# Three weight tables selected on VectorE in attention slots, and GpSimd's rotary sums ordered behind a slot's first scores

## The chip, the cores and the metric

The kernel runs on one core of a Trainium2 chip. Time is device time in microseconds (us) of one execution; the kernel before took 619.77 us, the median of three runs (619.49 to 621.18). A profiled execution of the same kernel took 619.1 us. All engine times below are from that execution, counted from the start of its span.

## The reference

Two transformer layers on a sequence tensor of 2 x 512 x 256, all in float32. Every sublayer is `x = x + layernorm(f(layernorm(x)))`:

```python
# layer 0: causal attention, 16 heads of 128, rotary embedding on q and k
q, k = rope(x @ wq.T + bq), rope(x @ wk.T + bk)
attn = softmax(where(causal, -inf, q @ k.T / sqrt(128)))
h = (attn @ v) @ wo.T + bo + residual
# layer 0 feed-forward, 256 -> 2048 -> 256: weights in 4-bit codes with a scale for each 32
W = NVFP4_LUT[codes] * scales;  out = (gelu(x @ Wg.T) * (x @ Wu.T)) @ Wd.T
# layer 1: linear attention with running sums over the sequence
out = q * cumsum(k * v) / (q * cumsum(k) + 1e-9) @ W_out.T / 4
# layer 1 feed-forward, 256 -> 688 -> 256: each weight is one of 16 values
w = lut[idx];  out = (silu(x @ wg.T) * (x @ wu.T)) @ wd.T
```

The change concerns the last line: the three tables `wg`, `wu`, `wd`, each `lut[idx]` with 16 possible values, have to be built on the chip from their index arrays before the last feed-forward.

## The kernel before, in words

**Stages.** Both batches of 512 positions are normalised (`first_norms`), then attention runs as 32 *slots*, one for each batch and head (`slot`, slot i is head i mod 16 of batch i div 16). After slot 17 and after slot 33 the sums over heads are finished and normalised; then come the first feed-forward for four units of 256 positions (`ffn_hidden`, `ffn_out`), linear attention (`linear_attention`) and the last feed-forward (`silu_hidden`, `silu_out`). Slots 30 to 33 already carry parts of the first `ffn_hidden`.

**What a slot does.** On TensorE (PE), in this order: the scores of head i, the projections of q and k for head i + 2, the output projection of head i - 2, the product of turned probabilities and values for head i - 1 (`attended`), and values for later heads. On VectorE (DVE): four reductions with the mask (`scores`, which writes the row minima `mn` and copies the scores into `p`), then the rotary products of q (`ra`, `ry`), the reciprocal of the row sums, the rotary product `ry` of k, and the four transposes of `p` into `turned`. On ScalarE (ACT): four exponentials, then `ra` of k, then the scaling of `p` by the reciprocals (four `p<-p,rs`), then two small copies that prepare a later slot's PSUM, then `oT` and `v`. On GpSimd (POOL): the sums `qT`, `kT` of the head after this one, and `ra*cos` of k. From slot 5 on, q and k of a head are projected two slots ahead, and their sums are made one slot ahead; for heads below 5 all is nearer together, and slot 3 makes the projections of k for head 4 and of q and k for head 5.

**Queues.** SyncE (SP) issues every DMA, in program order, each waiting in that queue for its own inputs. In a slot these are weight loads (`load`), the halves of `ry` exchanged into `rr`, and four DMAs `pT<-turned`, which bring the turned probabilities into place and can't start before `attended` of the slot has finished reading `pT` (one buffer).

**Dequantisation.** Twelve jobs turn 4-bit codes into weights of the first feed-forward (`dequantised`): a load of the codes `pk` (256 KB) and of the scales `sc`; then three steps, put into `behind` and taken out one at a time by `catch_up`: ACT casts `pk` to bytes `p8`; DVE separates the bits; DVE multiplies by the scales. Before the change the loads are issued in the middle of an even slot (from slot 2), the cast comes at that slot's end, the bits early in the next slot behind the scores, and the product at its end.

**The tables.** `wg` is built by `look_up_in`: for each of two pieces of 752 columns and 16 values, DVE makes `(idx == i) * lut[i]` and POOL adds it to the table; one such term per slot and a few more late. `wu` and `wd` are built by `select_in`, on DVE alone: for each piece 19 steps, which are 4 bit masks, 8 pairs (one of two table words by the lowest bit) and 7 predicated copies. `wu` (5 pieces of 256 columns) starts at slot 17, `wd` (3 pieces of 512) behind attention. These steps are *fills*: the recording layer `Engine` keeps a rough model of when each engine is busy, and where the model sees DVE idle ahead of its next instruction, it puts fills in front of that instruction; `flush` writes all that are left.

The order of instructions on each engine is thus fixed when the program is recorded: by the order of the code, by `poll` and `catch_up`, and by the model for the fills. On the chip every engine takes its instructions in that order.

Of the kernel before, what the change touches and what calls it, by code (L numbers as in the profile page):

```python
# [10 lines left out]
F32 = mybir.dt.float32  # L11
I32 = mybir.dt.int32
# [5 lines left out]
ALU = mybir.AluOpType  # L18

P = 128  # L20
HALF = P // 2
B = 2
S = 512
D = 256
# [18 lines left out]
SWAPPED = (1, 2)  # L43
WARM = 9
FROM = 5
REST = INTER - (NO - 1) * P


# [53 lines left out]
class Engine:  # L102
# [32 lines left out]
    def fill(self, until):  # L135
        self.filling = True
        while self.fills:
            us, reads, write = self.fills[0]
            if self.busy + us > until or (reads is not None and self.times.written(reads) > self.busy):
                break  # L140
            self.fills.popleft()
            write()
        self.filling = False

    def flush(self):
# [47 lines left out]
def sandwich_kernel(  # L193
# [58 lines left out]
    def begin(chain, delay=0.0):  # L252
        chains.append([now[0] + delay, chain])
# [13 lines left out]
    def catch_up():  # L267
        if behind:
            behind.popleft()()
# [171 lines left out]
        yield 0.0 if (u, stage) == (2, 1) else until(to)  # L441


    terms = deque()

    def look_up_in(scratch, pieces):


        n = [to.shape[-1] for _, to in pieces]
        ix = [scratch[:, 3 + j % 2, : n[j]].bitcast(I32) for j in range(len(pieces))]  # L450

        def fetch(j):
            if j < len(pieces):
                sync.dma_start(out=ix[j], in_=pieces[j][0])

        fetch(0)

        def term(j, i):
            if i == 2:
                fetch(j + 1)  # L460
            to = pieces[j][1]
            e = to if i == 0 else scratch[:, i % 3, : n[j]]
            vector.tensor_scalar(
                e, ix[j], float(i), lut_sb[:, i : i + 1], ALU.is_equal, ALU.mult
            )
            if i:
                pool.tensor_add(to, to, e)

        terms.extend(lambda j=j, i=i: term(j, i) for j in range(len(pieces)) for i in range(16))

    def select_in(scratch, pieces):


# [50 lines left out]
        fetch(0)  # L524
        for j in range(len(pieces)):
            vector.fills.extend(piece(j))

    def look_up(n):
        for _ in range(min(n, len(terms))):
            terms.popleft()()  # L530


    wg_u, wu_u, wd_u = [], [], []
    xT1 = [None] * NUNIT
    with ExitStack() as at:
# [319 lines left out]
            jobs.append((down_p, down_s, u, "d", w))  # L855
            wd_u.append(w)

        scratch = fh.tile([P, 5, wg.shape[-1]], F32, tag="hT", name="scratch", bufs=1)
        look_up_in(scratch, [(gate_i[:, kc, :], wg[:, kc, :]) for kc in range(NK)])
        words = lut_sb.bitcast(I32).rearrange("p (i j) -> p i j", j=2)  # L860

        p_at = [0, 128, 384, 768]
# [13 lines left out]
        def projection(kind, i, tag="mm"):  # L876


            b, h = divmod(i, NH)
            gg, hh = divmod(i, HG)  # L880
            w = wts[kind, gg]
            bias = col(kind, h)
            a = qk.tile([P, S], F32, tag="ra", name="ra", bufs=4)
            r = qk.tile([P, S], F32, tag="rr", name="rr", bufs=3)
            to = qk.tile([P, S], F32, tag=f"T{kind}", name=f"{kind}T", bufs=3)
            lo, hi = slice(0, 64), slice(64, 128)

            if i >= FROM:
                ps = bank(tag)
                for kc in range(NK):  # L890
                    matmul(
                        ps,
                        w[:, hh, kc, :],
                        chunk(xT0[b], kc) if b else xT0[b][:, kc, :],
                        kc == 0,
                        kc == NK - 1,
                    )
                yield
                y = qk.tile([P, S], F32, tag="ry", name="ry")
                if kind == "q":  # L900
                    vector.scalar_tensor_tensor(a, ps, bias, cos_sb, ALU.add, ALU.mult)
                else:
                    scalar.activation(a, ps, AF.Identity, bias=bias)
                    pool.tensor_mul(a, a, cos_sb)
                vector.scalar_tensor_tensor(y, ps, bias, sin_sb, ALU.add, ALU.mult)
                for half, other in ((lo, hi), (hi, lo)):
                    sync.dma_start(out=r[half], in_=y[other])
                yield
                pool.tensor_add(to, a, r)
                (qT if kind == "q" else kT)[i] = to  # L910
                return


            for cs in [slice(0, TU), slice(TU, S)] if i == 0 else [slice(0, S)]:
                ps = bank(tag)
                first_half = i == 0 and cs.start == 0
                tiles = [slice(0, P), slice(P, TU)] if first_half and kind == "q" else [cs]
                for n, (ts, kc) in enumerate((ts, kc) for ts in tiles for kc in range(NK)):
                    matmul(
                        ps[:, ts],  # L920
                        w[:, hh, kc, :],
                        chunk(xT0[b], kc) if b else xT0[b][:, kc, ts],
                        kc == 0,
                        kc == NK - 1,
                    )
                    if first_half and (kind, n) in (("q", 1), ("k", 0)):
                        yield
                yield
                def by_scalar():
                    scalar.activation(a[:, cs], ps[:, cs], AF.Identity, bias=bias)  # L930
                    pool.tensor_mul(a[:, cs], a[:, cs], cos_sb[:, cs])


                if i and (kind == "k") == (i > 1):
                    by_scalar()
                elif not first_half:
                    vector.scalar_tensor_tensor(
                        a[:, cs], ps[:, cs], bias, cos_sb[:, cs], ALU.add, ALU.mult
                    )
                vector.scalar_tensor_tensor(  # L940
                    r[lo, cs], ps[hi, cs], bias[hi], sin_sb[hi, cs], ALU.add, ALU.mult
                )
                vector.scalar_tensor_tensor(
                    r[hi, cs], ps[lo, cs], bias[lo], sin_sb[lo, cs], ALU.add, ALU.mult
                )
                if first_half:
                    by_scalar()
            yield
            if (kind, i) == ("k", 1):
                inverted(0)  # L950
            (pool if i > 1 or kind == "q" else vector).tensor_add(to, a, r)
            (qT if kind == "q" else kT)[i] = to
# [223 lines left out]
        def slot(i):  # L1176
# [11 lines left out]
                load("k", (i + 3) // 2)  # L1188
            if i == 4:
                vector.tensor_tensor(differ, words[:, :, 0], words[:, :, 1], ALU.bitwise_xor)  # L1190
            if i == NH + 2:
                attention_sums(0)
                begin(after_attention(0))
            if i == NH + 1:

                flat = [
                    [t.rearrange("p k c -> p (k c)") for t in (up_i, wu)],
                    [t[0].rearrange("p k s -> p (k s)") for t in (xT0, xTv)],
                ]
                parts = [[t[:, at : at + TU] for at in range(0, t.shape[-1], TU)] for t in flat[1]]  # L1200
                select_in(
                    parts[0] + parts[1],
                    [tuple(t[:, at : at + TU] for t in flat[0]) for at in range(0, NK * FULL * P, TU)],
                )
            now_in, done = i < NS, not (jobs or behind)
            if now_in:
                ps_p[i] = (
                    pr.tile([P, 1280], F32, tag="p", name="p"),
# [28 lines left out]
                exps(i, 2)  # L1237
                exps(i, 0)
                exps(i, 1)
            catch_up()  # L1240
            if i < NS - 2:
                look_up(i > 0)
            else:
                assert not terms
            turning = []
            if FROM <= i + 1 < NS:
                for kind in "qk":
                    next(begun.pop((kind, i + 1)), None)
            for kind in "qk":
                if kind == "q" and i in (0, 2, 3):  # L1250
                    pass
# [11 lines left out]
                elif i <= NS:  # L1263
                    next(main)
                    next(main)
                if kind == "q" and jobs and i % 2 == 0 and i >= 2:
                    dequantised(*jobs.popleft())
                if kind == "q" and i and now_in:
                    inverted(i)
            for work in turning:  # L1270
# [38 lines left out]
            elif NS - 2 < i <= NS:  # L1309
                next(main)  # L1310
                next(main)
            poll()
            if i < NS - 2:
                look_up(done)
            catch_up()

        pair = projection("q", 0), projection("k", 0, "o")
        for rows, cs, base in (
# [27 lines left out]
        for i in range(NS + 2):  # L1346
            slot(i)
        attention_sums(1)
        begin(after_attention(1))


# [8 lines left out]
    wout_sb = lw.tile([P, NK, D], F32, name="wout_sb")  # L1360
    sync.dma_start(out=wout_sb, in_=wout)
    carry = {}
    scratch = lw.tile([P, 8, 2 * D], F32, name="scratch2")
    vector.flush()
    select_in(
        [scratch[:, j] for j in range(8)],
        [
            tuple(t[:, o : o + 2, :].rearrange("p o d -> p (o d)") for t in (down_i, wd))
            for o in range(0, NO, 2)
        ],  # L1370
    )

    def linear_attention(u):
        def flat(t):
# [306 lines left out]
```

## Time and profile before

| what | us |
|---|---|
| time, median of three runs | 619.77 |
| time of the profiled execution | 619.1 |
| its span | 617.3 |
| PE busy | 610.4 (99% of the span) |
| DVE busy | 441.0 (71%) |
| ACT busy | 306.5 (50%) |
| POOL busy | 279.3 (45%) |
| POOL adding terms to `wg` | 53.7 (30 of 1.79 each) |
| DVE making those terms | 19.3 (32 of 0.604 each) |

The span is what the profiler records; the execution's own time is 1.8 us more. A busy time counts the union of an engine's instructions; they overlap a little, so the step from one start to the next is shorter than the duration of one. In the tables of groups, each line names an engine, an operation, `out<-in` by tile names, the count and the mean of one. In a timeline each line is `start, duration, engine, line, operation, out<-in`, and in brackets the idle time ahead of it and what ended it.

### The profile page before, as it was taken

What the parts mean: (1) busy time and instruction counts of PE and PEld (TensorE: products, weight loads), DVE (VectorE), ACT (ScalarE), POOL (GpSimd) and SP (SyncE); (2) the same over time, 40 slices, a digit from 0 to 9 for tenths busy, and PEclk for the clock granted to TensorE, in tenths of its full rate; (3) what the DMA queues carried; (4) which work ended last, traced back from release to release, by engine and by line L of the source; (5) the groups of instructions that cost most, each with busy time, mean ns of one, the idle gap of its engine ahead of it and who ended that gap; (6) DMA issues with size and microseconds to landing.
All of it is one profiled execution on the core that took longest, in us unless ns stands there. A gap on an engine that the chain in (4) does not pass through costs nothing.

```text
span 617.3 us, 13497 instructions
## 1 busy us (share of the span) xinstructions
PE 610.4 (99%) x4968; PEld 455.4 (74%) x4968; DVE 441.0 (71%) x1115; ACT 306.5 (50%) x716; POOL 279.3 (45%) x346
## 2 busy tenths in 40 slices
PE   9999999999999999999999999999999999999996
PEld 6455565555555566666777999999999999996664
DVE  7987778667665887887866788778986751562963
ACT  5665776677565666666656562132324223325110
POOL 6354666537456275675667300350261350161531
PEclk9999999999999999999999999999999999999999
DMA  8476777787877888788775432211001000001010
GB/s 224 141 199 171 206 191 201 193 234 199 196 214 194 202 212 194 189 216 215 192 169 138 101 70 60 104 36 35 1 8 31 1 18 18 2 1 35 19 53 18
DMA packets 53104, 75.60 MB, mean 122 GB/s; under 512 B 6960, under 2 KB 34096, under 8 KB 53040
## 3 DMA queue, kind: packets, MB, share of 16 engines
q1 hardware_dynamic: 53040, 74.76, 47.5%
q8 instruction: 39, 0.64, 0.4%
q14 instruction: 25, 0.20, 0.1%
HBM read 28.59 MB, written 1.05 MB: 48 GB/s over the span
## 4 chain that ended last, share of the span: by engine, by line
PE 97%; DVE 2%; ACT 1%; DMA 0%; issue 0%; POOL 0%; DVEq 0%
PE ps_mm L284 39%; PE ps_o L284 22%; PE ps_s L284 21%; PE ps_t L284 14%; DVE rr L185 0%; ACT p L185 0%; DMA x<-in_x_turned 0%; DVE p L185 0%; DVE x L185 0%; POOL rstd L185 0%; DVE st L185 0%; DVE ra L185 0%; DVE centred L185 0%; ACT ra L185 0%; DVE wg L185 0%
## 5 line engine op out<-in xcount | busy, mean ns | idle before, releaser
L185 POOL TENSOR_TENSOR wg<-wg,scratch 128x752 f32<-128x752 f32 x30 | 53.7, 1791 | 105.8 <-DVE scratch L185 74.1
L284 PE MATMUL ps_mm<-xT,wg 128*64 128x256 f32 (+1 forms) x704 | 89.0, 379 | 0.0
L284 PE MATMUL ps_s<-xT,wu 128*64 128x256 f32 x672 | 85.0, 379 | 0.0
L185 ACT ACTIVATE p<-p,mn 128x512 f32<-128x512 f32 (+3 forms) x128 | 70.3, 550 | 26.9 <-DVE mn L185 26.9
L284 PE MATMUL ps_o<-wd,hT 128*64 128x256 f32 (+1 forms) x704 | 77.1, 375 | 0.0
L284 PE MATMUL ps_t<-pT,v 128*64 128x256 f32 (+3 forms) x512 | 75.5, 432 | 0.0
L284 PEld LDWEIGHTS ps_mm<-xT,wg 128*64 128x64 f32 (+1 forms) x704 | 71.2, 137 | 5.6 <-ACT si L185 0.4
L284 PEld LDWEIGHTS ps_o<-wd,hT 128*64 128x64 f32 x704 | 68.8, 137 | 6.3
L284 PEld LDWEIGHTS ps_s<-xT,wu 128*64 128x64 f32 x672 | 69.0, 137 | 4.5 <-DVE hT L185 0.3
L185 DVE CUSTOM_DVE_ANT_0 p<-ps_s,mask 128x512 f32<-128x512 f32 x64 | 31.3, 489 | 52.6 <-PE ps_s L284 49.3
L284 PEld LDWEIGHTS ps_t<-pT,v 128*64 128x64 f32 x512 | 45.9, 137 | 30.8 <-issue 22.4
L185 ACT ACTIVATE p<-p,rs 128x512 f32<-128x512 f32 (+3 forms) x128 | 61.1, 550 | 2.4 <-DVE rs L185 2.4
L284 PE MATMUL ps_o<-wo,oT 128*64 128x256 f32 x512 | 62.0, 379 | 0.0
L284 PEld LDWEIGHTS ps_o<-wo,oT 128*64 128x64 f32 x512 | 46.2, 137 | 21.1 <-issue 14.2
L284 PE MATMUL ps_mm<-xT,wk 128*64 128x512 f32 x248 | 59.4, 592 | 1.0 <-DVE rr L185 1.0
L284 PE MATMUL ps_mm<-xT,wq 128*64 128x512 f32 (+2 forms) x256 | 59.9, 577 | 0.1
L284 PE MATMUL ps_s<-kT,qT 128*64 128x64 f32 (+5 forms) x384 | 57.1, 424 | 0.0
L284 PE MATMUL ps_mm<-wv,xTv 128*64 128x256 f32 x464 | 55.9, 379 | 0.0
L185 DVE SCALAR_TENSOR_TENSOR ry<-ps_mm,cols_sb,sin_sb 128x512 f32<-128x512 f32 x54 | 40.3, 746 | 20.7 <-ACT ra L185 20.7
L185 DVE STREAM_TRANSPOSE turned<-p 128x512 f32<-128x512 f32 (+3 forms) x128 | 53.8, 476 | 0.3 <-ACT p L185 0.2
L185 POOL TENSOR_TENSOR ra<-ra,cos_sb 128x512 f32<-128x512 f32 (+1 forms) x33 | 46.0, 1395 | 16.5 <-ACT ra L185 16.5
L284 PEld LDWEIGHTS ps_s<-kT,qT 128*64 128x64 f32 x384 | 34.8, 137 | 23.7 <-issue 13.1
(162 smaller groups left out, 951.1 us busy)
## 6 DMA issues: line engine op xcount, KB each, us to landing
pT<-turned SPq DMA_DIRECT2D x128, 208.0 KB, 4.0
rr<-ry SPq DMA_DIRECT2D x108, 128.0 KB, 2.5
wo<-in_wo SPq DMA_DIRECT2D x17, 256.0 KB, 4.2
wv<-in_wv SPq DMA_DIRECT2D x16, 256.0 KB, 3.9
wq<-in_wq SPq DMA_DIRECT2D x15, 256.0 KB, 4.2
wk<-in_wk SPq DMA_DIRECT2D x15, 256.0 KB, 4.5
xT<-tr SPq DMA_DIRECT2D x48, 64.0 KB, 2.1
pk_g<-in_gate_p SPq DMA_DIRECT2D x4, 256.0 KB, 3.7
```

What stands on the lines that cost most here:

```text
L185: return write(*args, **more)
L284: nc.tensor.matmul(out[part], lhsT=lhsT[:, part], rhs=rhs, start=start, stop=stop, **more)
```

## The change

`look_up_in` and its terms on POOL are gone. All three tables go through `select_in`: `wg` and `wu` from slot 4 on in pieces of up to 512 columns (three for `wg`, three for `wu`), with a scratch tile of 8 x 512; `wd` from the end of slot 28 in six pieces of 256, with tiles of the first batch as scratch. Besides the places that the model sees as idle, fills are now forced at the end of each slot until the model's DVE is busy to 2.4 us beyond the model's time (`force`, `AHEAD`), and what is left is flushed at the end of slot 28 and behind attention. The loads of a dequantisation job and its steps move: loads at the end of an even slot, cast behind the next slot's exponentials (`if len(behind) == 3`), bits at the end of that slot, product at the end of the slot after. On POOL a small instruction that reads the first reduction's `mn` stands ahead of the two sums. `ra` has three buffers and not four.

```diff
+AHEAD = 2.4
...
+    def force(self, until):
+        self.filling = True
+        while self.fills and self.busy + self.fills[0][0] <= until:
+            self.fills.popleft()[2]()
+        self.filling = False
...
-    terms = deque()
-
-    def look_up_in(scratch, pieces):
...
-            vector.tensor_scalar(
-                e, ix[j], float(i), lut_sb[:, i : i + 1], ALU.is_equal, ALU.mult
-            )
-            if i:
-                pool.tensor_add(to, to, e)
...
-        scratch = fh.tile([P, 5, wg.shape[-1]], F32, tag="hT", name="scratch", bufs=1)
-        look_up_in(scratch, [(gate_i[:, kc, :], wg[:, kc, :]) for kc in range(NK)])
...
-            a = qk.tile([P, S], F32, tag="ra", name="ra", bufs=4)
+            a = qk.tile([P, S], F32, tag="ra", name="ra", bufs=3)
...
             if i == 4:
                 vector.tensor_tensor(differ, words[:, :, 0], words[:, :, 1], ALU.bitwise_xor)
+                scratch = fh.tile([P, 8, S], F32, tag="hT", name="scratch", bufs=1)
+                pieces = []
+                for codes, to in ((gate_i, wg), (up_i, wu)):
+                    codes, to = (t.rearrange("p k c -> p (k c)") for t in (codes, to))
+                    n = to.shape[-1]
+                    pieces += [tuple(t[:, at : min(at + S, n)] for t in (codes, to)) for at in range(0, n, S)]
+                select_in([scratch[:, j] for j in range(8)], pieces)
...
-            if i == NH + 1:
...
-                select_in(
-                    parts[0] + parts[1],
-                    [tuple(t[:, at : at + TU] for t in flat[0]) for at in range(0, NK * FULL * P, TU)],
-                )
...
-            catch_up()
-            if i < NS - 2:
-                look_up(i > 0)
-            else:
-                assert not terms
-            turning = []
+            if len(behind) == 3:
+                catch_up()
             if FROM <= i + 1 < NS:
+                after = small.tile([P, 1], F32, tag="after", name="after", bufs=1)
+                pool.tensor_scalar(after, ps_p[i][1][:, NT - 1 :], 1.0, None, ALU.mult)
                 for kind in "qk":
                     next(begun.pop((kind, i + 1)), None)
+            turning = []
...
-                if kind == "q" and jobs and i % 2 == 0 and i >= 2:
-                    dequantised(*jobs.popleft())
...
             poll()
+            catch_up()
+            if jobs and i % 2 == 0 and i >= 2:
+                assert not behind
+                dequantised(*jobs.popleft())
             if i < NS - 2:
-                look_up(done)
-            catch_up()
+                vector.force(now[0] + AHEAD)
+            if i == NS - 4:
+                vector.flush()
+                flat = [t[0].rearrange("p k s -> p (k s)") for t in (xT0, xTv)]
+                select_in(
+                    [t[:, at : at + TU] for t in flat for at in range(0, t.shape[-1], TU)],
+                    [(down_i[:, o, :], wd[:, o, :]) for o in range(NO)],
+                )
...
+        vector.flush()
         begin(after_attention(1))
...
-    scratch = lw.tile([P, 8, 2 * D], F32, name="scratch2")
-    vector.flush()
-    select_in(
-        [scratch[:, j] for j in range(8)],
...
-    )
```

More of the change, by code (lines that the diff above doesn't have):

```diff
@@ L441, in norms @@
         yield 0.0 if (u, stage) == (2, 1) else until(to)
-    terms = deque()
-    def look_up_in(scratch, pieces):
[L449 to L462, printed above, removed]
-            vector.tensor_scalar(
-                e, ix[j], float(i), lut_sb[:, i : i + 1], ALU.is_equal, ALU.mult
-            )
-            if i:
-                pool.tensor_add(to, to, e)
-        terms.extend(lambda j=j, i=i: term(j, i) for j in range(len(pieces)) for i in range(16))
     def select_in(scratch, pieces):
@@ L526, in select_in @@
             vector.fills.extend(piece(j))
-    def look_up(n):
-        for _ in range(min(n, len(terms))):
-            terms.popleft()()
     wg_u, wu_u, wd_u = [], [], []
@@ L1193, in slot @@
                 begin(after_attention(0))
-            if i == NH + 1:
[L1196 to L1200, printed above, removed]
-                select_in(
-                    parts[0] + parts[1],
-                    [tuple(t[:, at : at + TU] for t in flat[0]) for at in range(0, NK * FULL * P, TU)],
-                )
-            now_in, done = i < NS, not (jobs or behind)
+            now_in = i < NS
             if now_in:
@@ L1362, in sandwich_kernel @@
     carry = {}
-    scratch = lw.tile([P, 8, 2 * D], F32, name="scratch2")
-    vector.flush()
-    select_in(
-        [scratch[:, j] for j in range(8)],
[L1367 to L1370, printed above, removed]
-    )
     def linear_attention(u):
```

## The prediction

> **What bounds the kernel now.** I read the page's busy times and the chain that ended last, then what PE waited for, then timelines of slots 3, 9, 10 and 25 on each engine, because the chain alone doesn't say how much room other engines have.
>
> ```profile
> PE 610.4 (99%) x4968; PEld 455.4 (74%) x4968; DVE 441.0 (71%) x1115; ACT 306.5 (50%) x716; POOL 279.3 (45%) x346
> ...
> PE 97%; DVE 2%; ACT 1%; DMA 0%; issue 0%; POOL 0%; DVEq 0%
> ...
> PE ps_mm L284 <- DVE rr L185: 1.0, 1, 1.0
> PE ps_o L581 <- PEq L1669: 0.8, 1, 0.8
> PE ps_t L284 <- ACT wu L185: 0.3, 1, 0.3
> ```
>
> PE is the bound. The last three lines are all that it ever waited for: 2.1 us, of which 1.0 is in slot 3. Freeing DVE or POOL can return almost nothing; the question is whether the new order makes PE wait. From slot 5 a slot takes 10.98 us; I count time in a slot from its first scores on PE. Slot 3, the one with the wait, in lines of the timelines of SP, ACT, DVE and PE, and the load's own time to landing:
>
> ```profile
> 45.08 0.60 SPq L167 DMA_DIRECT2D wq<-in_wq  x1
> ...
> wq<-in_wq SPq DMA_DIRECT2D x1, 256.0 KB, 4.0
> ...
> 44.05 0.62 ACT L185 CAST p<-pk_g 128x512 uint8<-128x512 int32 x1
> ...
> 47.35 0.67 ACT L185 ACTIVATE ra<-ps_mm,cols_sb 128x512 f32<-128x512 f32 x1
> ...
> 48.12 1.51 DVE L185 SCALAR_TENSOR_TENSOR rr<-ps_mm,cols_sb,sin_sb 64x512 f32<-64x512 f32 x2 [0.26 <-ACT ra L185]
> ...
> 49.78 1.94 PE L284 MATMUL ps_mm<-xT,wk 128*64 128x512 f32 x8 [0.99 <-DVE rr L185]
> ```
>
> PE waits for a PSUM bank that DVE's `rr` of k frees, and `rr` waits for ACT's `ra` of k. The cast is out of the way at 44.05. A 256 KB load issued right behind slot 2's pT DMAs lands 4.0 later. The same views of slots 9 and 10 (first scores at 112.05 and 123.03):
>
> ```profile
> 121.52 3.33 SPq L167 DMA_DIRECT2D pT<-turned  x4
> 124.89 3.18 SPq L167 DMA_DIRECT2D xT<-wd  x4
> 128.17 0.54 SPq L167 DMA_DIRECT2D wv<-in_wv  x1
> ...
> wv<-in_wv SPq DMA_DIRECT2D x1, 256.0 KB, 3.2
> ...
> 129.41 0.75 DVE L185 SCALAR_TENSOR_TENSOR ry<-ps_mm,cols_sb,sin_sb 128x512 f32<-128x512 f32 x1 [0.94 <-ACT ra L185]
> 130.08 1.68 DVE L185 STREAM_TRANSPOSE turned<-p 128x512 f32<-128x512 f32 x4
> ...
> 130.14 2.32 PE L284 MATMUL ps_t<-pT,v 128*64 128x512 f32 x16
> ```
>
> SP's pT DMAs start 9.47 into a slot, 0.83 apart, so the fourth starts at 11.97; with the 4.1 that late pT DMAs take it lands at 16.07, and PE wants pT at 10.98 + 7.11 = 18.09 (130.14). The transposes may slip about 2 us, no more. Here too `ry` of k waits for ACT's `ra`.
>
> **POOL's terms go, fills come.** The 30 additions (30 x 1.791 = 53.7 us) and 32 terms on DVE (32 x 0.604 = 19.3) go. Selection on 512 columns costs per step, start to start, 0.34 for a mask, 0.47 for a pair, 0.68 for a copy (rows of the `wd` selection around 425): 8.5 us for 19 steps. Three pieces for `wg` are 25 us, the `wu` pieces about as before, `wd` goes from three pieces to six of 256, about 6.5 each against 8.5. Counted by the changed program's order with these steps, DVE has 9.4 to 11.1 us of work in slots 8 to 17 against 8.3 at most before, slot 17 apart. This fits into 10.98 on average, so the load as such I cost at nothing; the cover is DVE's idle time before a slot's first reduction (3.43 us at 135.19, none of it on PE's path). If it were gone, a rival below.
>
> **POOL's sums behind `mn`.** What queues behind the new instruction is qT, kT and the product `ra*cos`; PE wants the sums at 10.98. The first reduction ends near 1.8, two sums take 2.56: done by 5 to 6.5. Cost 0. `ra` with three buffers makes ACT wait for the sum qT, done by 5, before 5.66. Cost 0.
>
> **The flush behind attention.** 34 steps of 256 columns, 13 copies of 0.43 and 21 others of about 0.3: 11.9 us of DVE, against 3.7 there before (388.57 to 392.25). The next `hT` product comes at 400.5; PE first needs its bank at 410.0, because 13.8 us of `ffn_out` lie between. Cost 0, with 9.5 in hand; the norms behind it are then due by 434 and ready by about 420. The tail after 540 keeps its order of DVE work and gains nothing.
>
> **The dequantisation loads, moved behind pT on SP.** This is the part that costs. The codes are now issued after the slot's four pT DMAs, and ACT's cast stands behind the exponentials and in front of `ra` of k. ACT takes its queue in order, so everything behind the cast waits for the load: `ra`, then DVE's `ry` of k, the scaling of p, the transposes and pT.
>
> *Slot 3.* The codes take the place that `wq` had: issue 45.08, landing 49.08. The cast takes 0.51 to the next start (135.43 to 135.94), so `ra` starts at 49.61 and not 47.35: +2.26, all on PE's path. Against it, slot 1 loses the term of 0.52 us in front of the rotary products, on the chain to PE's start at 28.34; PE itself is free at 26.35 + 1.73 = 28.08, so -0.26. Sum +2.0; with the smallest landing of `pk_g` (2.9) +0.9, with the largest behind pT (5.9) +3.9.
>
> *Slot 9 to 10.* At the end of slot 8 four DMAs `xT<-wd` also stand before the codes. pT(8) from 110.54, +3.33, +3.28 for the four: codes issued at 117.15, landed at 120.35 (3.2, as the load behind the same four). `ra` 120.9 to 121.5, `ry` to 122.3. Then the changed order has seven fills in front of the transposes: three masks 1.02, two pairs 0.94, two copies 1.36, sum 3.32, to 125.6. Transposes to 127.3, fourth pT DMA at 129.85, landed at 133.9. PE wanted it at 130.14: +3.8.
>
> *Slot 25 to 26.* The same with `xT<-tr` at the end of slot 24 (3.07 for four, then 2.8 to landing): pT(24) from 286.2, codes at 292.6, landed 295.4, `ry` to 297.4, ten fills (4.74) to 302.1, transposes to 303.8, fourth pT DMA at 306.4, landed 310.5, wanted at 298.72 + 7.11 = 305.83: +4.7.
>
> *The other odd slots to 23.* Codes issued at 1.85, landed at 5.95 (4.1, median behind pT), `ry` ends at 7.95; with F us of fills ahead of the transposes pT lands at 16.3 + F. F is 0.6 to 1.4, below the 1.8 left; in slot 21 it is 1.96 and the load there took 4.4: +0.4. For loads that land late I add 0.3 in all. Bounds: 0 (all early) and 3.
>
> Sum: 2.0 + 3.8 + 4.7 + 0.4 + 0.3 = 11.2. The profiled execution took 619.1 (span 617.3 and 1.8 around it), 0.67 under the median; 619.1 + 11.2 = 630.3, on the median 631.0.
>
> [...] Row: POOL's product `ra*cos`, usually 1.28, took 2.26 at 120.95 beside DVE's dequantising product. [...] That speaks against the fills, which now lie beside `ra*cos` in slots 9 and 25; if DVE lost there what POOL lost at 120.95, 0.98 each, the sum would be 13.2. I keep 11.2, since in that row it was POOL that stretched. [...]
>
> **Rivals.** *Hidden anyway (not slower):* the cast finds its codes there. This needs a landing within 47.35 - 0.51 - 45.08 = 1.8 us in slot 3, and in slots 9 and 25 pT 3.8 and 4.7 earlier than I have it. For it: ACT is only 50% busy. Against: the least that I found for a 256 KB load is 2.8. Price: -0.3 to +1.2, 619 to 621.
>
> *DVE becomes the bound:* slots 8 to 17 need about 100.5 of 109.8 us. For it: 256-wide pairs took 434 ns on average in attention and 365 to start unhindered; fills that are 1.45 times as long make 11.5 us a slot, 0.5 over, in some 20 slots +10 on top: 641. It decides from about 1 us more per slot. Against: POOL's 53.7 us are gone.
>
> *Gains win:* PE's wait in slot 3 and the 0.26 of slot 1 all returned, 1.3 us: 618.5. Against: `rr` there waits for ACT, not for the terms that go.
>
> **How the numbers follow.** No change and 0.3% (1.9 us) are about what a measurement can't tell apart. Late codes as summed: 0.74, 627 to 641 (0.9 + 2.4 + 3.7 + 0 = 7.0 on 619.77 at the low end, with the codes landing after 2.8 and pT after its least, 3.1; 3.9 + 6.5 + 7.8 + 3 = 21.2 at the high end, with the codes after 5.9). DVE bound: 0.15. Hidden: 0.08, nearly all within 0.3%. Gains: 0.03. Faster 0.02, same 0.08, slower 0.90. The range 623 to 642 leaves out the hidden case and the far end of the DVE case.
>
> **What would show it.** Right: PE idle before `ps_t<-pT,v` in slots 10 and 26, 3 to 6 us each, released by the DMA pT; PE's wait in slot 3 grown to about 3 us; ACT idle before casts, released by the codes' DMA; DVE's `ry` of k waiting for ACT up to 3 us longer in odd slots; PE unbroken after slot 33. Wrong: casts without idle time before them; or PE waits in most slots from 8 to 17, released by DVE (then the load decides, not the codes); or a wait at 400 to 415 (the flush).

## The result, and the profile after

The changed kernel takes 645.63 us (median of four runs, 641.67 to 647.55) against 619.63 us before: a ratio of 1.0407 with a 95% interval of 1.0355 to 1.0459. It is slower by 26 us. I had said 631.0 with a range of 623 to 642, so the direction was right and the size too small by more than half.

The profiled execution took 645.61 us, its span 643.8 against 617.3. From the page of the changed kernel, the busy times and the granted clock of TensorE in 40 slices, in tenths:

```profile
PE 619.3 (96%) x4968; PEld 392.6 (61%) x4968; DVE 456.0 (71%) x1159; ACT 304.7 (47%) x716; POOL 224.6 (35%) x343
...
PEclk9998999989999999999979999999999999999999
```

PE does the same 4968 matmuls, but they take 619.3 us and not 610.4, and it waits 19.6 us and not 2.0. The seven and the eights in the second line were nines before. What PE waited for, in the view of waits (total us, times, longest):

```profile
PE ps_t L291 <- DMA pT<-turned: 12.6, 8, 4.5
PE ps_mm L291 <- DVE rr L192: 3.1, 1, 3.1
PE ps_s L291 <- ACT ps_s L192: 1.8, 2, 1.1
PE ps_mm L291 <- DVE x L192: 1.1, 1, 1.1
```

The first two lines are the waits that the prediction named: for pT, and in slot 3 for `rr` of k. The third is ACT's copies of the mask, which stand behind the cast and the scalings. The chain of slot 9 into slot 10, in lines of the timelines of ACT, DVE, SP and PE:

```profile
125.70 0.62 ACT L192 CAST p<-pk_u 128x512 uint8<-128x512 int32 x1 [3.08 <-DMA pk_u<-in_up_p]
126.22 0.68 ACT L192 ACTIVATE ra<-ps_mm,cols_sb 128x512 f32<-128x512 f32 x1
...
126.94 0.75 DVE L192 SCALAR_TENSOR_TENSOR ry<-ps_mm,cols_sb,sin_sb 128x512 f32<-128x512 f32 x1 [4.11 <-ACT ra L192]
127.60 1.24 DVE L192 COPY_PREDICATED wg<-scratch 128x512 int32<-128x512 int32 x1
...
131.40 1.68 DVE L192 STREAM_TRANSPOSE turned<-p 128x512 f32<-128x512 f32 x4
...
133.14 3.19 SPq L174 DMA_DIRECT2D pT<-turned  x4
...
139.53 3.31 PE L291 MATMUL ps_t<-pT,v 128*64 128x512 f32 x16 [3.12 <-DMA pT<-turned]
```

ACT stands 3.08 us in front of its cast, `ra` comes behind it, DVE's `ry` waits 4.11 us for `ra`, seven selection steps take 127.60 to 131.40, then come the transposes and pT. The last line has one thing that the chain does not explain: these 16 matmuls took 3.31 us, and 2.32 before (130.14).

Set slot against slot, from one slot's first scores on PE to the next one's, the 26.5 us of span come apart like this. Idle time is read from the timeline of PE. For half clock I count half of the time in which PE worked at a granted clock of 0.50 (the 16 `ps_t<-pT,v` from 329.76, all at 0.50, took 4.53 us, and 2.35 at 1.00 from 123.95). The rest is what remains. "All else" is the start, slot 1, the tail and slots that changed by less than 0.1 us; in the tail the clock falls in both kernels only after PE's last matmul, so it costs PE nothing there. A stop at the first scores counts in the slot before them.

| slot | longer by | PE idle | half clock | rest |
|---|---|---|---|---|
| 3 | 3.84 | 2.14 | 1.71 | 0.00 |
| 9 and 10 | 6.30 | 1.06 + 3.12 | 1.71 | 0.41 |
| 25 and 26 | 8.52 | 0.74 + 4.54 | 2.81 | 0.43 |
| 8, 14, 17, 18, 20, 22, 24 | 8.31 | 6.19 | 0 | 2.12 |
| all else | -0.5 | -0.3 | 0 | -0.2 |
| sum | 26.5 | 17.5 | 6.2 | 2.8 |

The rest is about 0.2 us for each stop: slot 8 has one stop of 0.99 and is 1.20 longer; slot 20 has two, of 1.08 and 1.16, and is 2.69 longer. What it consists of I did not test.

The clock, in windows of 3.41 us whose edges are the moments at which the granted clock changed (columns: busy us of PE, PEld, DVE, ACT, POOL, each with its count; granted clock; DMA share; GB/s):

```profile
48.65:52.07 3.42, 0.45 (x2) 0.23 (x4) 2.07 (x3) 1.21 (x2) 1.72 (x2) 1.00 0.53 180
52.07:55.48 3.41, 3.41 (x13) 1.48 (x11) 0.84 (x2) 0.49 (x1) 0.82 (x1) 0.50 0.35 82
...
137.40:140.81 3.41, 1.28 (x8) 0.65 (x10) 3.16 (x6) 2.44 (x7) 1.35 (x2) 1.00 0.94 296
140.81:144.23 3.42, 3.42 (x20) 2.36 (x18) 3.38 (x7) 1.35 (x2) 0.00 (x0) 0.50 0.35 106
...
325.13:328.55 3.42, 0.09 (x2) 0.00 (x0) 3.02 (x11) 3.42 (x11) 3.20 (x4) 1.00 0.90 212
328.55:331.96 3.41, 2.20 (x6) 0.77 (x8) 3.21 (x9) 1.46 (x5) 0.92 (x2) 0.50 0.98 291
331.96:335.37 3.41, 3.41 (x20) 1.86 (x18) 3.27 (x9) 0.69 (x1) 1.60 (x1) 0.50 0.15 39
335.37:338.78 3.41, 3.41 (x30) 2.14 (x28) 1.49 (x6) 1.00 (x2) 0.36 (x2) 1.00 0.85 187
```

Three times PE worked little in a window (0.45, 1.28 and 0.09 us of 3.41), and each time the next window ran at 0.50. After slot 26 two windows did.

### The profile page after: what moved, and what is told of

Same layout as the page of the kernel before. It is cut to its first block, busy times and chain, and to the rows that moved or that the text cites. A ratio compares the mean times of both kernels' runs of the same rounds, so it can differ in the third digit from the quotient of the medians.

```text
span 643.8 us, 13518 instructions
## 1 busy us (share of the span) xinstructions
PE 619.3 (96%) x4968; PEld 392.6 (61%) x4968; DVE 456.0 (71%) x1159; ACT 304.7 (47%) x716; POOL 224.6 (35%) x343
## 4 chain that ended last, share of the span: by engine, by line
PE 74%; DMA 11%; DVE 5%; SPq 4%; ACT 3%; issue 2%; POOL 0%; DVEq 0%
PE ps_mm L291 28%; PE ps_s L291 17%; PE ps_o L291 17%; PE ps_t L291 11%; DMA pT<-turned 6%; SPq L174 4%; ACT p L192 2%; DVE turned L192 1%; DMA wk<-in_wk 1%; DMA rr<-ry 1%; DMA pk_u<-in_up_p 1%; DVE scratch L192 1%; DMA pk_g<-in_gate_p 1%; ACT ra L192 1%; DMA pk_d<-in_down_p 0%
## 5 line engine op out<-in xcount | busy, mean ns | idle before, releaser
L291 PE MATMUL ps_mm<-xT,wg 128*64 128x256 f32 (+1 forms) x704 | 85.8, 379 | 0.0
L291 PEld LDWEIGHTS ps_t<-pT,v 128*64 128x64 f32 x512 | 41.0, 141 | 53.1 <-issue 39.4
L291 PEld LDWEIGHTS ps_mm<-xT,wg 128*64 128x64 f32 (+1 forms) x704 | 54.5, 137 | 21.1 <-ACT si L192 0.4
L291 PEld LDWEIGHTS ps_o<-wd,hT 128*64 128x64 f32 x704 | 54.1, 137 | 20.9
L192 DVE TENSOR_TENSOR hT<-ge,ps_s 128x512 f32<-128x512 f32 x32 | 21.8, 685 | 61.2 <-PE ps_s L291 36.9
L291 PEld LDWEIGHTS ps_s<-xT,wu 128*64 128x64 f32 x672 | 52.3, 137 | 20.3 <-DVE hT L192 0.3
L192 POOL TENSOR_TENSOR ra<-ra,cos_sb 128x512 f32<-128x512 f32 (+1 forms) x33 | 41.0, 1245 | 61.5 <-ACT ra L192 61.4
L291 PE MATMUL ps_s<-kT,qT 128*64 128x320 f32 (+5 forms) x384 | 57.6, 424 | 1.8 <-ACT ps_s L192 1.8
L291 PEld LDWEIGHTS ps_o<-wo,oT 128*64 128x64 f32 x512 | 40.9, 138 | 27.9 <-issue 15.2
L192 ACT ACTIVATE ln<-x,shift,rstd 128x256 f32<-128x256 f32 x22 | 13.2, 606 | 77.3 <-POOL shift L192 76.6
```

The lines of the kernel that those rows point to most:

```text
L192: return write(*args, **more)
L291: nc.tensor.matmul(out[part], lhsT=lhsT[:, part], rhs=rhs, start=start, stop=stop, **more)
```

## The experiments

Three things can be the cause: the late codes with the cast that waits for them (the prediction's theory, A), the selection's steps in the slots (B), or GpSimd's sums behind the row minima (C). What is undone or moved in each run is told against the changed kernel, except where the text names another. (The expectations call the reductions that make `mn` the row maxima.)

### The codes back in the middle of the even slots

```diff
-            if len(behind) == 3:
-                catch_up()
+            catch_up()
...
+                if kind == "q" and jobs and i % 2 == 0 and i >= 2:
+                    dequantised(*jobs.popleft())
...
-            if jobs and i % 2 == 0 and i >= 2:
-                assert not behind
-                dequantised(*jobs.popleft())
```

> The changed kernel with one part undone: the dequantisation's loads and its three steps go back to the middle of the even slots, as before the change; selection, GpSimd's sums and all the rest stay as changed. Theory A (ACT's cast that waits for the late codes starts every stop of TensorE; half clock and restarts only follow from the stops): the stops in slots 8, 10, 14, 17, 18, 20, 24 and 26 go, TensorE's idle time falls from 19.6 to 1-3 us, its clock stays at 1.00 up to the tail, the time is 617-621 us. Rival B (the selection's steps in front of the transposes make p late by themselves, whatever the codes do): slots 10 and 26 keep stops of 3-5 us and their half clock, 630-640 us. Rival C (GpSimd's sums behind the first scores are the cause): the cast is early but kT is late, stops at the scores, over 625 us.

Measured: 629.8 us (ratio 1.0159, 1.0144 to 1.0174), span 628.6. The stops in slots 10 and 26 are gone and the clock stays at 1.00 up to the tail, but 7.6 us of stops are left beside those of before, all in odd slots from 5 to 19:

```profile
PE ps_t L291 <- DMA pT<-turned: 3.0, 5, 1.3
PE ps_mm L291 <- DVE rs L192: 2.7, 5, 1.1
PE ps_s L291 <- ACT ps_s L192: 1.9, 6, 0.3
```

Neither A (617 to 621) nor B, as worded, fits. DVE and POOL in slot 13, from the timelines:

```profile
165.62 0.67 DVE L192 TENSOR_SCALAR pk_u<-p 128x128 int32<-128x128 int32 x1
166.21 1.31 DVE L192 TENSOR_SCALAR c<-p 128x128 int32<-128x128 int32 x1
167.55 0.29 DVE L192 TENSOR_TENSOR c<-c,pk_u 128x128 int32<-128x128 int32 x1
167.76 1.29 DVE L192 TENSOR_SCALAR c<-p 128x128 int32<-128x128 int32 x1
...
164.92 1.28 POOL L192 TENSOR_TENSOR qT<-ra,rr 128x512 f32<-128x512 f32 x1
166.16 1.27 POOL L192 TENSOR_TENSOR kT<-ra,rr 128x512 f32<-128x512 f32 x1
167.64 1.33 POOL L192 TENSOR_TENSOR ra<-ra,cos_sb 128x512 f32<-128x512 f32 x1 [0.21 <-ACT ra L192]
```

A bit step of 0.22 us takes 1.3 and ends when POOL's instruction ends (166.29 against 166.20, 167.52 against 167.43, 169.05 against 168.97). Over the kernel the 24 `c<-p` steps took 897 ns on average and 220 before (groups of this run and of the kernel before; busy us and mean ns behind the bar):

```profile
L192 DVE TENSOR_SCALAR c<-p 128x128 int32<-128x128 int32 x24 | 21.5, 897 | 0.0
L185 DVE TENSOR_SCALAR c<-p 128x128 int32<-128x128 int32 x24 | 5.3, 220 | 0.0
```

So a second coupling, D: in these rows a bit step beside POOL's instruction lasts to about that instruction's end, and the change puts POOL's sums where the bit steps were. What holds the step there is not shown.

### The late codes alone, in the kernel before

The same edit the other way round, made in the kernel before.

> The kernel before with one part of the change alone: the dequantisation is queued at the end of the even slots and its cast stands behind the next slot's exponentials; the look-up by terms, GpSimd's sums and the rest as before. Theory A with the fills as a second factor: the casts start 5.7-8.9 us into the odd slots as in the changed kernel, p is late by the same wait, but only one look-up term stands in front of the transposes; slot 3 stops for about 3 us with one half-clock window behind it (1.7 us), slots 10 and 26 for 0.3-1.0 us each, the small stops give 2-4 us: 626-632 us. If the late codes do all of it without the fills: 640 us and more. If they do nothing without the fills: 619-621 us.

Measured: 624.14 us (1.0068, 1.0054 to 1.0082), span 621.0. Slot 3 has its stop:

```profile
PE ps_mm L284 <- DVE rr L185: 3.1, 1, 3.1
```

and slots 10 and 26 have 0 and 0.3 us. So without the selection in front of the transposes, late codes cost 4.5 us, less than I expected. In the profiled execution slot 3 has 2.1 of the 3.6 us that the span grew. The clock did not fall behind this stop of 3.1 us (the mean granted clock was 1.0): it lay across two windows, idle for 49% of one and 42% of the other.

### The selection cut to two steps of 19

The pieces of `wg` and `wu` keep only their first mask and first pair; the other 17 steps are left out, so these two tables are not looked up.

```diff
+                if full or i in (0, 2)
...
-                select_in([scratch[:, j] for j in range(8)], pieces)
+                select_in([scratch[:, j] for j in range(8)], pieces, full=False)
```

> The changed kernel with 17 of the 19 steps of each piece of the gate and up selection left out (these two tables are then not looked up, and the outputs are wrong); late codes and all else as changed, so that hardly a fill stands in front of the transposes (at most two in slots 5 to 8, none from slot 9 to 28). Theory A with the fills as a second factor: the stop before the attended matmuls shrinks from 4.2 to about 0.5 us in slots 9 to 10 and from 5.3 to 0.5-1.0 us in slots 25 to 26, their half clock goes, slot 3 keeps its 3.1 us and one half-clock window: 626-632 us. Rival B (selection is the whole cause): 619-622 us, slot 3 without its stop. If the codes alone do it: 640 us and more.

Measured: 627.26 us (1.0118, 1.0089 to 1.0147), as expected from A with the fills as a second factor. In the profiled execution slot 3 is 3.94 us longer (2.24 idle, 1.71 half clock), slots 9 to 10 are 0.8 and slots 25 to 26 are 1.2. B as the whole cause falls, and so do the codes alone: in the spans the late codes alone cost 3.6 us, the rest of the change with early codes 11.3, and all together 26.5.

### PE kept busy in its two long stops

```diff
             po = bank("t")
+            for _ in range({9: 2, 25: 3}.get(i, 0)):
+                for at in range(0, P, HALF):
+                    nc.tensor.matmul(
+                        po[at : at + HALF], lhsT=ident[:, at : at + HALF], rhs=cos_sb, start=True, stop=True
+                    )
             for jt in range(NT):
```

> The changed kernel with TensorE kept busy in its two long stops: two products of ident with cos_sb (128x512, 1.9 us) in front of the attended matmuls of slot 10 and three (2.9 us) in front of those of slot 26, into the bank that these overwrite. The data come no sooner. If it is the idle time of TensorE that halves its clock: no half clock behind slots 10 and 26, 1.7 and 2.8 us less there, 640-642 us; slot 3, left as it was, keeps its half-clock window of 3.41 us. If the clock falls for another reason (power, the traffic): 645-646 us with the same windows.

Measured: 640.26 us (1.0346, 1.0314 to 1.0377), 5.4 us less than the changed kernel, though PE was given five more products. The windows with the stops of slots 3, 10 and 26, and the one behind each, on the grid of that run, columns as above:

```profile
49.37:52.78 3.41, 1.36 (x8) 0.62 (x10) 2.91 (x4) 0.35 (x1) 2.53 (x2) 1.00 0.56 200
52.78:56.19 3.41, 3.41 (x28) 2.14 (x26) 2.02 (x4) 2.70 (x6) 1.28 (x1) 1.00 0.37 87
...
134.70:138.11 3.41, 2.42 (x16) 0.87 (x11) 3.01 (x7) 3.41 (x11) 3.07 (x3) 1.00 0.91 236
138.11:141.52 3.41, 2.89 (x24) 1.89 (x26) 3.41 (x8) 1.23 (x5) 0.00 (x0) 1.00 0.82 261
141.52:144.94 3.42, 3.42 (x32) 2.44 (x30) 3.39 (x8) 2.80 (x5) 0.07 (x1) 1.00 0.71 134
...
322.43:325.85 3.42, 2.55 (x12) 0.67 (x8) 3.02 (x11) 3.42 (x11) 3.21 (x3) 1.00 0.91 212
325.85:329.26 3.41, 2.20 (x16) 1.13 (x18) 3.09 (x8) 1.33 (x5) 0.80 (x2) 1.00 0.94 314
329.26:332.68 3.42, 3.42 (x34) 2.23 (x32) 3.28 (x9) 1.27 (x2) 1.60 (x1) 1.00 0.55 92
```

In this execution no window ran at half clock up to the tail. Without the products the window from 134.70 would have been idle for some 85% and the one from 322.43 throughout (an estimate from where the products lay: 1.91 us from 135.21, 2.77 from 322.21); with them PE was idle for 29 and 25%. The DMA share there, 0.91, is about that of the windows in which the changed kernel lost its clock (0.94 and 0.90). So in these runs it is PE's idle time, and not the traffic, that goes with the half clock. Two things limit this. Slot 3, which I had left alone, kept its clock too, in spite of a stop of 2.9 us: the first line shows that PE was busy for 1.36 us of the window. And the slowest of the four executions (644.69 us) had a mean clock of 0.991 and not 0.998 or more, so the clock did not hold in each.

### The bit steps behind the transposes, codes early

Against the first run of this section: the bits and the product by the scales both come at the end of the odd slot.

```diff
-            catch_up()
             if FROM <= i + 1 < NS:
...
             catch_up()
+            if odd:
+                catch_up()
```

> The changed kernel with the codes' loads and cast back in the middle of the even slots (as in the run with the codes back), but VectorE's five bit steps and the scaling by sc behind the odd slot's transposes instead of between the row maxima and the rotation. Theory D (in the run with the codes back, the 11 us that stay are the bit steps held up by GpSimd's sums of q and k, which the change puts at the same place: 897 instead of 220 ns each): the steps go back to about 0.2 us each, no stop of TensorE is left but those of before, 617-621 us. Rival B (the selection's forced steps at the slots' ends delay the row maxima by about 2 us, and that is enough for stops): 625-630 us, with stops in odd slots.

Measured: 620.65 us (1.0015, 1.0004 to 1.0025), span 617.9. D holds, and B falls for good: the whole selection, forced steps included, lies in this kernel, and PE's stops are 0.4 and 0.2 us beyond those of before. Out of POOL's way the bit steps are worth 9.2 us (629.8 to 620.65). Moving them also takes five steps of 0.2 to 0.3 us out from in front of the rotation; the kernel before had them there, and PE had no stop in slots 5 to 19.

### Codes back, and GpSimd's wait for `mn` taken out

```diff
-                after = small.tile([P, 1], F32, tag="after", name="after", bufs=1)
-                pool.tensor_scalar(after, ps_p[i][1][:, NT - 1 :], 1.0, None, ALU.mult)
```

> The changed kernel with the codes back in the middle of the even slots and GpSimd's wait for the row maxima taken out too, so that GpSimd sums q and k as soon as their parts have landed; selection as changed. Theory D: the bit steps in the odd slots take 0.2-0.3 us each again, and the stops of 0.6-1.4 us in slots 5 to 19 go; the sums now fall on the forced selection steps at the slots' ends, which become longer, with 1-3 us of their own: 618-623 us. Rival B: 627-631 us as with the codes back alone.

Measured: 636.11 us (1.0266, 1.0236 to 1.0295), 6.3 more than with the wait, and 13 more than I allowed for. The bit steps did come down (310 ns), but now POOL's sums fall on the selection steps at the slots' ends. From the groups, where the last numbers before the idle time are busy us and mean ns:

```profile
L192 DVE COPY_PREDICATED scratch<-scratch 128x512 int32<-128x512 int32 x16 | 17.4, 1085 | 0.3
L192 DVE TENSOR_SCALAR scratch<-scratch 128x512 int32<-128x512 int32 x16 | 12.5, 797 | 0.6 <-DMA scratch<-in_gate_i 0.6
```

They took 778 and 491 ns in the first run, with the wait, and 747 and 415 in the kernel before, where they ran behind attention. The timelines of the changed kernel show what lies beside a long one: the ten rows of one selection step of 128x512 that are above 0.9 us there (seven copies of 1.24 to 1.28, three other steps of 0.93 and 0.94) each overlap POOL's `ra*cos`. The expectation had the longer steps right and a price of 1 to 3 us, where 12.4 us of idle time came of it. This run also shows how little idle time went with a half clock:

```profile
144.62:148.03 3.41, 1.40 (x12) 0.63 (x10) 3.34 (x15) 2.77 (x10) 0.95 (x2) 1.00 0.89 278
148.03:151.45 3.42, 3.42 (x17) 1.95 (x15) 3.27 (x7) 2.34 (x7) 1.11 (x2) 0.50 0.71 152
```

PE was busy for 1.40 us and the next window ran at half clock; with 1.36 us, in slot 3 of the run with PE kept busy, it did not.

### One line: the cast behind the scalings

```diff
-            if len(behind) == 3:
-                catch_up()
...
                     scalar.mul(pi, pi, rs[i][:, it : it + 1])
+            if len(behind) == 3:
+                catch_up()
```

> The changed kernel with one line moved: ACT's cast of the codes stands behind the four scalings of p in the odd slots instead of behind the exponentials; the late loads, the selection and GpSimd's sums stay as changed. Theory A (the cast that waits for the codes in front of ra and the scalings is what makes p late, and the fills stand in front of the transposes because the schedule has p late too): slots 3, 10 and 26 lose their stops of 2.1, 4.2 and 5.3 us and the half clock, and so do the small stops: TensorE idle 1-3 us, 617-622 us. If the late landing holds something else up (bit steps, the mask copies behind the cast on ACT), or the forced fills are enough by themselves: 625-635 us.

Measured: 620.49 us (1.0016, 1.0006 to 1.0026), span 617.7. In slots 9 and 25 the codes are issued as late as in the changed kernel (4.82 and 5.53 us into the slot, 4.83 and 5.33 there), in the other odd slots from 5 to 23 at 1.83 to 2.67. 25 of its 26 us are gone; PE's waits from slot 3 on are these two:

```profile
PE ps_mm L291 <- DVE rr L192: 0.9, 1, 0.9
PE ps_mm L291 <- DMA wq<-in_wq: 0.6, 1, 0.6
```

ACT and DVE in slot 9, from the timelines:

```profile
117.96 0.66 ACT L192 ACTIVATE ra<-ps_mm,cols_sb 128x512 f32<-128x512 f32 x1
118.53 1.91 ACT L192 ACTIVATE p<-p,rs 128x512 f32<-128x512 f32 x4
120.34 0.60 ACT L192 CAST p<-pk_u 128x512 uint8<-128x512 int32 x1
...
119.33 1.68 DVE L192 STREAM_TRANSPOSE turned<-p 128x512 f32<-128x512 f32 x4
```

`ra` goes first, the cast finds its codes there, and in slots 9 and 25 the recorded order has no fill and one fill in front of the transposes instead of seven and ten. One moved line changed that order, so the model, too, must have seen p come late behind the cast and put fills there. The second factor is a consequence of the first.

### The same, with GpSimd's wait for `mn` taken out

The edit of the sixth run, made in this kernel.

> The kernel with the cast behind the scalings (620.5 us), and GpSimd's wait for the row maxima taken out, so that its sums of q and k run as soon as their parts have landed and fall on the selection's steps at the slots' ends. If such steps are held up by GpSimd's sums whatever the codes do (with codes and sums back, a copy_predicated of 128x512 took 1085 against 747 ns, a tensor_scalar 797 against 415): the row maxima come 2-3 us later, stops of 0.3-1.5 us in a good many slots, 625-635 us. If the hold was a matter of the bit steps in the odd slots alone: 619-622 us.

Measured: 633.92 us (1.0256, 1.0226 to 1.0286). The copies of 128x512 take 1007 ns and PE is idle for 9.4 us more than before. The wait on GpSimd, which I had costed at nothing, is worth 13.4 us beside forced fills.

### Fewer forced steps

The kernel with the bit steps behind the transposes, with `AHEAD = 2.0`.

> The kernel with early codes and the bit steps behind the transposes (620.65 us), with the selection's forced steps let run 2.0 instead of 2.4 us past the end of a slot. If its two small stops (0.36 us in slot 5, 0.17 in slot 13) come from forced steps in front of the row maxima: they go, span 617.0-617.4, time 619.0-620.0, within 0.2% of before on either side. TensorE's own 610 us of matmuls leave no more to gain by any placing of VectorE's and GpSimd's work. If the steps left over for the flush behind slot 28 (14 of them, 7 us) hold up slot 29: a stop there and 620-622 us.

Measured: 619.88 us (1.0000, 0.9991 to 1.0009), span 618.1. The stop of slot 13 went, that of slot 5 stayed (0.6 us), one of 0.3 us came up in slot 25, and the steps left to slot 28 did no harm. It equals the kernel before and does not beat it: PE's 610 us (610.4 busy before, 610.8 in the one-line run) are its floor too.

## Why the prediction was right about the sign and wrong about the size

*PE is the bound, freed time returns nothing.* Right. With the cast behind the scalings POOL is busy for 225.6 us instead of 279.3, the whole selection runs on DVE, and the time is 0.16% longer than before.

*Terms go and fills come: 0.* Right for the load on DVE, and the rival that DVE becomes the bound is refuted: the same selection fits beside a PE that is 99% busy. That this rival's 641 us lies nearest to the result says nothing for it; nor does its factor of 1.45 follow from the 434 and 365 ns beside it, which give 1.19.

*The flush behind attention, the third buffer of `ra`: 0.* Right; PE doesn't wait behind slot 33.

*POOL's sums behind `mn`: 0.* Right in this kernel, but for a reason that I had not seen. The look-up terms before had kept POOL off DVE's bit steps. In slot 9 of the kernel before, the bit steps ended at 116.06, DVE's term came behind them, POOL's addition waited for the term, and qT for the addition:

```profile
115.98 0.61 DVE L185 TENSOR_SCALAR scratch<-scratch,lut_sb 128x752 f32<-128x752 int32 x1
...
116.73 1.79 POOL L185 TENSOR_TENSOR wg<-wg,scratch 128x752 f32<-128x752 f32 x1 [6.53 <-DVE scratch L185]
118.47 1.28 POOL L185 TENSOR_TENSOR qT<-ra,rr 128x512 f32<-128x512 f32 x1
```

From a single row, in which POOL stretched, I took DVE to be safe. The run with the codes back shows DVE held up instead: bit steps of 0.22 us took up to 1.31 beside sums of 1.28. In the changed kernel itself this costs little, as the bits had moved away: the copy at 127.60 took 1.24 and not 0.75 us beside POOL's product, and the seven and ten fills in front of the transposes took 3.80 and 5.15 us where I had 3.32 and 4.74. The 0.98 each that I had weighed and left out would have been too much.

*Codes behind pT, the cast in front of `ra`: 11.2.* The mechanism is shown by the one-line run. The large terms were near: slot 3 +2.26, measured 2.14 of idle time, and slot 1 -0.26, measured -0.31 in length (together the +2.0 of the sum); slot 9 to 10 +3.8, measured 1.06 + 3.12 = 4.18, of which the 1.06 was at the scores of slot 10, behind ACT's copies of the mask, a place I had not named; slot 25 to 26 +4.7, measured 5.28.

The sum failed at three of its terms:

1. *"For loads that land late I add 0.3 in all"*, with 0.4 for slot 21, for the other odd slots. Measured 6.2 us of idle time, outside my bound of 3. The step that failed is that I priced each odd slot by itself, with every load issued 1.85 into the slot and landed at 5.95. The codes were issued at 1.74 to 3.40 (slot 11 apart) and the casts started at 5.7 to 8.2, because a delay carries into the next slots. In slot 16, for one, DVE's bit steps and seven selection steps stood behind the late transposes, and the first reduction started 4.0 us into the slot (1.2 before); so pT left at 211.85, and the codes of slot 17 stood behind it in SP's queue, at 215.22. With late codes and without the selection, in the second run, the stops other than slot 3's came to 0.3 us. Of the 6.2 us, 1.3 were in waits for DVE (`h` and `x`) and not for pT.
2. *Half clock: no term at all*, 6.2 us. The chain of 11.2 took stops of more than 3 us as if only their length counted.
3. *Restart after a stop: no term*, 2.8 us, about 0.2 a stop.

With these three, the 10.5 for slot 1 and the large stops (measured 11.3) would have come to some 26. Setting the codes' landing by rows held to within a us: in slot 9 they were issued at 4.83 and cast at 8.85, in slot 7 at 2.65 and 6.64, 4.0 us each, where I had taken 3.2 and 4.1 to the landing.

## What to carry to other kernels

In a queue that an engine takes in order, an instruction that waits for a late load belongs behind everything that is due sooner; here that place was worth 25 us and the late load itself next to nothing. A stop of TensorE cost its length here, plus about 0.2 us, plus 1.7 us for each busy window of 3.41 us at half clock behind it, so a forecast needs all three terms; products put into two of the stops were worth 5.4 us. Before moving GpSimd work, look at which VectorE instructions will lie beside it: here bit steps of 0.22 us, which earlier work had kept apart from GpSimd's sums of 1.28 us, took up to 1.31 beside them.

## What the runs showed of the hardware that I had not expected

In the changed kernel the granted clock went to 0.50 for one or two steps of 3.413 us: from 52.07, 140.81 and 328.55, which are 26 and 55 such steps apart, though the stops ahead of them began at 48.49, 136.41 and 325.22. A window at full clock in which PE was idle for 62, 87 or 97% (this kernel) or 59% (codes and sums back) was followed by one at half clock; at 60% (slot 3 of the run with PE kept busy), 49% (late codes alone) and 34% and less (this kernel) it was not (the ends of matmuls are modelled, so one per cent either way decides nothing). So a stop of 3 us cost 1.7 us more or nothing, it seems by where it fell: slot 3 stopped for 2.9 to 3.2 us in four of the profiles and lost its clock in two. By an estimate this accounts for much of the changed kernel's spread: its quickest run (span 639.8) had a mean clock of 0.993 against 0.988 in the profiled one (643.8). Over 640 us at half rate that is some 6.4 us at 0.50, about two windows, 3.2 of the 4.0 us between them. A window at half clock that was idle for 36%, in slot 26, was followed by another at half clock.

A 128x128 tensor_scalar on VectorE grew from 220 to 1310 ns beside a GpSimd sum, ending within 0.1 us of it (codes back), and a copy_predicated of 128x512 from 747 to 1085 ns on average (codes and sums back).
